# Seven block products for eight in the last MLP layer of a two-layer graph network

## Chip, cores, metric

The kernel runs on one core of a Trainium2 chip. The metric is the device time of one execution in microseconds; the figure given is the median over runs. The profile shown is of one profiled execution.

## The reference

3327 nodes with 1024 features each and a weighted adjacency matrix go through two residual layers. The first normalises the rows, quantises them, multiplies by a quantised weight and then by the adjacency matrix. The second is a graph attention with 8 heads of 64 features, followed by an MLP. Only the end of it is touched here:

```python
enc = jnp.transpose(h, (1, 0, 2)).reshape(x.shape[0], -1)   # 3327 x 512
out = jax.nn.relu(enc @ W1.T + b1)                          # 256
out = jax.nn.relu(out @ W2.T + b2)                          # 256
out = jax.nn.relu(out @ W3.T + b3)                          # 512
out = out @ W4.T + b4                                       # 1024
...
x = x + _L1_gnn_ref(h, adj, ...)
```

All of it is float32. The last product is 3327 x 512 times 512 x 1024, and its result is added to the layer's input, which the kernel calls x1.

## The kernel before

**Stages.** The kernel works through the network in stages: the first layer's support, its product with the adjacency matrix together with the heads of the second layer, the attention (`acc`, `mps`, lines 785 to 1156), and the MLP (lines 1159 to 1257). The nodes lie in 26 tiles of 128 rows, the last with 127 real ones. The MLP takes them in groups of four tiles: six groups of four and one of two.

**A layer of the MLP.** `dense` (line 1166) keeps the features on the partitions and has the nodes of a group as up to 512 columns. For each of the layers h1, h2, h3 TensorE multiplies 128 x 128 blocks of the weight with the group's activations (8, 4 and 8 matmuls), and ScalarE takes each sum out of PSUM with bias and relu (line 1186). Group 0 has its first layer computed inside the last step of the attention.

**The last layer.** `rows_out` (line 1200) makes the output rows of one node tile. Here `h3` is the stationary side (128 features by 128 nodes) and `w4` the moving one (128 by 512 outputs), so the result has nodes on the partitions. Two column halves of 512 and four blocks of features make 8 matmuls. VectorE adds the bias `bb4` to the rows of x1 (line 1201), and then the sums in PSUM to that (line 1205); SyncE's queue sends the rows out (line 1207). A tile's two halves share one PSUM tile of two banks, and there are two such tiles; only the last node tile is taken by halves.

**The order of the work.** The matmuls of the next group's layers h1, h2, h3 are placed between the last-layer products of the current group's tiles by the loop at line 1236, so that ScalarE's activations are done before TensorE needs them. x1 for the next group comes from memory by `load_x1` into one of two buffers, `nodes0` and `nodes1`; `joined` loads the attention's output by a transposing DMA and puts its two 16-bit halves together with four ScalarE copies a group (`enct`, line 1197). Engines take their instructions strictly from a list that a scheduler has ordered at build time: what stands later in an engine's list waits for what stands earlier.

**The seam between attention and MLP.** The last reader of the attention's mask is `sel` (line 1109) on VectorE. Then the last head is closed (lines 924 to 969): sums and a division on VectorE (`su`, L936, L941, L943; `rs`, L946), scaling and an exponential on ScalarE (L939, L949, L951, L952), a last VectorE step `ht` (L956), ScalarE's copy `eh` (L962), and two DMAs to `enc_d` that GpSimd's queue issues (L964). In the same microseconds TensorE computes h2 and h3 of group 0 and ScalarE takes them out.

**Buffers.** `weights` holds the four weights, `rest` the biases and group 0's first layer with its input `enct0`, and `mask1` is the attention's second mask, which is no longer read when the MLP runs.

The softmax here doesn't subtract the row's maximum and nothing guards it: scores larger than these inputs give would overflow.

## Time and profile before

| What | Value |
|---|---|
| Time, median of 3 runs (lowest to highest) | 2207.7 us (2207.35 to 2208.68) |
| Span of the profiled execution | 2207.1 us |
| Clock granted to TensorE | full, mean 1.000 |
| First matmul of h2, group 0 | 1918.2 us |
| First weight load of the last layer | 1929.0 us |
| Last matmul ends | about 2202.6 us |
| 2010 to 2160 us: busy, in us of 150 | PE 150.00, DVE 30.76, ACT 25.17, POOL 0.00 |
| The same stretch, data moved | 85 GB/s |

The profiled execution is known by its span, from the first instruction to the last; the median of the runs lies 0.6 us above it. PE is TensorE, PEld its weight loads, DVE VectorE, ACT ScalarE, POOL GpSimd, SP SyncE. The page gives each engine's busy time, then the span in 40 slices (a digit is the busy share in tenths), then the chain that ended last, followed back from the last instruction, and the costliest groups of instructions: line, engine, operation, output and inputs, shape and count, then busy time and the mean duration in ns, then the engine's idle time ahead of them with what ended it. The timeline gives start and duration in us and the same names. Ends of matmuls are modelled, so their spacing says more than their duration. What the prediction shows of these is not repeated here.

### The profile page before, as it was taken

How to read it: one execution, taken by the hardware profiler on the slowest of the kernel's cores; microseconds unless marked ns; L12 is line 12 of the kernel's file. 1: busy time of each engine (PE TensorE's matmuls, PEld its weight loads, DVE VectorE, ACT ScalarE, POOL GpSimd, SP SyncE). 2: the span in 40 equal slices, each digit the busy share in tenths (PEclk: the TensorE clock that was granted, in tenths of full speed). 3: DMA queues.
4: the chain of work that ended last, by engine and by line, in shares of the span. 5: the costliest groups of instructions: out<-in, count | busy, mean ns of one | idle time of the engine just before them, and what ended most of it. 6: DMA issues, size and time to landing. Idle time of an engine off the chain costs nothing.

```text
span 2207.1 us, 31283 instructions
## 1 busy us (share of the span) xinstructions
PE 2173.1 (98%) x12457; PEld 1747.8 (79%) x12457; DVE 1542.5 (70%) x2000; ACT 1112.0 (50%) x1715; POOL 176.2 (8%) x269
## 2 busy tenths in 40 slices
PE   5999999999999999999999999999999999999999
PEld 2477777776777777799999999999999999744444
DVE  8745555555455555779999999999999999822211
ACT  6734445544455444566555565555555555532110
POOL 2301000111101101100000000000000000000000
PEclk9999999999999999999999999999999999999999
DMA  6654565555655556944242422644242432372221
GB/s 219 165 186 152 160 193 179 171 168 158 185 186 179 164 159 187 322 126 148 87 150 79 146 87 74 221 146 148 85 150 87 138 91 78 103 209 86 97 84 67
DMA packets 242433, 321.13 MB, mean 145 GB/s; under 512 B 104868, under 2 KB 186996, under 8 KB 242288
## 3 DMA queue, kind: packets, MB, share of 16 engines
q1 hardware_dynamic: 221676, 245.91, 36.6%
q0 software_dynamic: 20544, 73.18, 10.6%
q8 instruction: 97, 1.59, 0.3%
q14 instruction: 48, 0.39, 0.1%
q10 hardware_dynamic: 68, 0.06, 0.0%
HBM read 208.72 MB, written 86.79 MB: 134 GB/s over the span
## 4 chain that ended last, share of the span: by engine, by line
PE 89%; DVE 5%; DMA 3%; ACT 1%; issue 1%; SPq 0%; POOL 0%; DVEq 0%; ACTq 0%; POOLq 0%
PE acc L1134 29%; PE mm L730 24%; PE mps L883 15%; PE o L1216 8%; PE whm L641 7%; PE h_ps L1176 5%; PE mm L337 2%; DMA at<-in_adj_t 1%; DMA yht<-yh 1%; DVE sel L1109 1%; DMA xqt<-xq 0%; DVE stats L250 0%; DVE lo L189 0%; DMA w<-in_w 0%; PE o_half L1216 0%
## 5 line engine op out<-in xcount | busy, mean ns | idle before, releaser
L1109 DVE SCALAR_TENSOR_TENSOR sel<-srow,ndst,mask 128x896 fp32r<-128x896 f32 (+1 forms) x832 | 865.2, 1084 | 40.4 <-PE acc L1134 34.8
L883 PE MATMUL mps<-dw,mf 128*128 128x260 f32 x2704 | 453.7, 283 | 0.0
L730 PE MATMUL mm<-s_int,hi 128*128 128x512 f32 x1352 | 426.3, 396 | 0.0
L730 PE MATMUL mm<-s_int,lo 128*128 128x512 f32 x1352 | 416.6, 389 | 0.0
L1134 PE MATMUL acc<-f_even,sel 128*128 128x260 f32 x2704 | 396.8, 284 | 0.7 <-DVE sel L1109 0.7
L1134 PE MATMUL acc<-f_odd,sel 128*128 128x260 f32 x2704 | 394.1, 286 | 0.4 <-DVE sel L1109 0.4
L876 ACT CAST mf<-mask 128x1664 fp32r<-128x1664 uint8 x208 | 331.5, 1594 | 112.6 <-PE mps L883 98.3
L883 PEld LDWEIGHTS mps<-dw,mf 128*128 128x128 f32 x2704 | 377.9, 188 | 0.2 <-ACT part L897 0.2
L1134 PEld LDWEIGHTS acc<-f_odd,sel 128*128 128x128 f32 x2704 | 352.8, 188 | 7.8 <-issue 3.4
L1134 PEld LDWEIGHTS acc<-f_even,sel 128*128 128x128 f32 x2704 | 354.8, 188 | 4.2 <-DVE sel L1109 1.3
L730 PEld LDWEIGHTS mm<-s_int,hi 128*128 128x128 f32 x1352 | 253.9, 188 | 62.5 <-issue 11.5
L730 PEld LDWEIGHTS mm<-s_int,lo 128*128 128x128 f32 x1352 | 253.7, 188 | 52.9 <-DVE lo L189 0.2
L189 DVE TENSOR_TENSOR lo<-at,hi 128x896 fp32r<-128x896 f32 x104 | 106.2, 1021 | 157.3 <-ACT hi L185 157.3
L641 PE MATMUL whm<-whead,ht 128*128 128x512 f32 x416 | 182.7, 592 | 0.0
L1216 PE MATMUL o<-weights,h 128*128 128x512 f32 x400 | 174.8, 592 | 0.0
L190 DVE TENSOR_SCALAR mk<-at 128x896 uint8<-128x896 f32 (+1 forms) x104 | 61.5, 593 | 142.9 <-DMA at<-in_adj_t 142.9
L185 ACT CAST hi<-at 128x896 fp32r<-128x896 f32 x104 | 92.2, 887 | 130.1 <-PE mm L730 94.8
L1216 PEld LDWEIGHTS o<-weights,h 128*128 128x128 f32 x400 | 76.0, 190 | 94.4 <-issue 94.0
L641 PEld LDWEIGHTS whm<-whead,ht 128*128 128x128 f32 x416 | 78.8, 190 | 89.1 <-issue 87.1
L897 ACT COPY part<-mps 128x260 f32<-128x260 f32 x103 | 39.0, 378 | 190.1 <-PE mps L883 190.1
L964 POOL DMA_DIRECT2D enc_d<-eh x64 | 57.6, 903 | 907.0 <-ACT eh L962 906.5
L1186 ACT ACTIVATE h<-h_ps,rest 128x512 f32<-128x512 f32 (+1 forms) x54 | 34.9, 653 | 180.5 <-PE h_ps L1176 180.5
(175 smaller groups left out, 1676.4 us busy)
## 6 DMA issues: line engine op xcount, KB each, us to landing
feat_d<-fw POOLq DMA_DIRECT2D x26, 1040.0 KB, 5.3
f_even<-feat_d SPq DMA_DIRECT2D x7, 3380.0 KB, 13.5
f_odd<-feat_d SPq DMA_DIRECT2D x7, 3380.0 KB, 12.7
at<-in_adj_t SPq DMA_DIRECT2D x52, 448.0 KB, 4.2
at<-in_adj_t SPq DMA_DIRECT2D x52, 384.0 KB, 4.1
dw<-dsum_d SPq DMA_DIRECT2D x16, 910.0 KB, 8.8
dsum_d<-dw POOLq DMA_DIRECT2D x26, 520.0 KB, 6.2
x_d<-xt POOLq DMA_DIRECT2D x26, 512.0 KB, 6.7
```

Source lines behind the costliest of these rows:

```text
L185: ins = nc.scalar.copy(hi, at)
L189: nc.vector.tensor_tensor(lo, at, hi.bitcast(F32), ALU.subtract)
L190: ins = nc.vector.tensor_scalar(mk[:, r], at, 0.0, None, ALU.is_gt)
L641: ins = nc.tensor.matmul(whm, ht[:, k, :], whead[:, k, :], start=(k == 0), stop=(k == KF - 1))
L730: nc.tensor.matmul(mm[:, c * 512 : (c + 1) * 512], which[:, q, :], s_int[j][:, c * 512 : (c + 1) * 512], start=(j == 0 and which is hi), s ...
L876: ins = nc.scalar.copy(mf, mask[:, j : j + TH, :])
L883: nc.tensor.matmul(ps, mf[:, j % TH, :], dw[:, j, :], start=(j == 0), stop=(j == T - 1))
L964: nc.gpsimd.dma_start(enc_d[q, sub[0] * P : (sub[-1] + 1) * P, h * HD : (h + 1) * HD].rearrange("(b p) d -> p b d", p=P), eh[:, q].rearran ...
L1109: ins = nc.vector.scalar_tensor_tensor(sel[:, :nb], srow[:, :nb], ndst[:, j, h : h + 1], mask[:, :, j, :], ALU.is_gt, ALU.mult,)
L1134: ins = nc.tensor.matmul(accs[b], sel[:, b, :], f[:, j, :], start=(j == 0), stop=(j == T - 1))
L1176: ins = nc.tensor.matmul(pss[m][:, :cols], wt[:, k, m * P : (m + 1) * P], xt[:, k, :cols], start=(k == 0), stop=(k == k_n - 1),)
L1216: nc.tensor.matmul(ps, h3[:, k, q * P : (q + 1) * P], w4[:, k, cs], start=(k == 0), stop=(k == D3 // P - 1),)
```

## The change

The last layer is computed for two node tiles at once. The two tiles' features, split in two halves of 256, make a 2 x 2 block matrix (a11, a12; a21, a22); the weight, split in two halves of features and two of outputs, makes another. Their product by Winograd's form of Strassen's scheme needs seven block products and fifteen block sums in place of eight products.

- Four block sums of the weight are made once, by GpSimd, 128 x 1024 elements each: t1 over a quarter of `w4` itself, t2, t3, t4 in the memory of `mask1`. Each takes the one before it, or is ordered with it by the place it overwrites.
- Four block sums of the features are made for each group by VectorE (`combined`), s1 to s4, 512 columns each, in the memory of `enct0`; one set of buffers for all groups.
- A product is two matmuls into one PSUM bank of 512 columns. There are four banks in rotation in place of two tiles of two.
- Seven block sums join the products to output blocks, in `rows_out`: VectorE adds into the x1 rows or into `kept`, three of the products are first copied out of PSUM by ScalarE. Rows leave in halves of 512 columns, four DMAs a pair in place of two.
- The next group's layers stand at other places, between the products of a pair (`at`).

```diff
-    ) as ps_p, tc.tile_pool(name="s4_o", bufs=2, space=PSUM, reuse_waits="tile") as o_ps:
+    ) as ps_p, tc.tile_pool(name="s4_o", bufs=4, space=PSUM, reuse_waits="tile") as o_ps:
...
-        def rows_out(t, x1, h3, q, halfway=lambda: None):
-            nc.vector.tensor_tensor(x1[:, q, :], x1[:, q, :], bb4, ALU.add)
-            yo = s4.tile([P, F], F32, name="yo")
-
-            def leave(c, sums):
-                nc.vector.tensor_tensor(yo[:, c], sums, x1[:, q, c], ALU.add)
+        w4c = [[w4[:, 2 * k : 2 * k + 2, c * 512 : (c + 1) * 512] for c in range(FC)] for k in range(2)]
+        t2, t3, t4 = (
+            masks[1].rearrange("p b j i -> p (b j i)").bitcast(F32)[:, n * F : (n + 1) * F].rearrange(
+                "p (k c) -> p k c", k=2
+            )
+            for n in range(3)
+        )
+        t1 = w4c[0][1]
+        nc.gpsimd.tensor_tensor(t3, w4c[1][1], w4c[0][1], ALU.subtract)
+        nc.gpsimd.tensor_tensor(t1, w4c[0][1], w4c[0][0], ALU.subtract)
+        nc.gpsimd.tensor_tensor(t2, w4c[1][1], t1, ALU.subtract)
+        nc.gpsimd.tensor_tensor(t4, w4c[1][0], t2, ALU.subtract)
+        sums = enct0.rearrange("p k c -> p (k c)").rearrange(
+            "p (s k t i) -> p s k t i", s=4, k=2, t=2
+        )
+
+        def combined(h3, n):
+
+            at = h3[:, :, : 2 * n * P].rearrange("p k (t e i) -> p k t e i", e=2, i=P)
+            (a11, a21), (a12, a22) = [[at[:, 2 * k : 2 * k + 2, :, e] for e in range(2)] for k in range(2)]
+            s1, s2, s3, s4_ = (sums[:, q, :, :n] for q in range(4))
+            nc.vector.tensor_tensor(s1, a21, a22, ALU.add)
+            nc.vector.tensor_tensor(s2, s1, a11, ALU.subtract)
+            nc.vector.tensor_tensor(s3, a11, a21, ALU.subtract)
+            nc.vector.tensor_tensor(s4_, a12, s2, ALU.subtract)
+            return {
+                "1": (a11, w4c[0][0]),
+                "2": (a12, w4c[1][0]),
+                "3": (s4_, w4c[1][1]),
+                "4": (a22, t4),
+                "5": (s1, t1),
+                "6": (s2, t2),
+                "7": (s3, t3),
+            }
+
+        def rows_out(tiles, x1, of, q, gaps):
...
+            for e in range(2):
+                nc.vector.tensor_tensor(x0[:, e], x0[:, e], bb4, ALU.add)
...
+            yo = [s4.tile([P, F], F32, name="yo", bufs=3) for _ in tiles]
+
+            def leave(e, c, one, other):
+                t, cs = tiles[e], slice(c * 512, (c + 1) * 512)
+                nc.vector.tensor_tensor(yo[e][:, cs], one, other, ALU.add)
                 for queue, r in zip((nc.sync, nc.scalar), row_pieces(t)):
...
+                    queue.dma_start(out[t * P + r.start : t * P + r.stop, cs], yo[e][r, cs])
+
+            kept = {b: s4.tile([P, 512], F32, name="p" + b, bufs=1) for b in "165"}
+            for n, b in enumerate("1426573"):
+                st, mv = of[b]
+                ps = o_ps.tile([P, 512], F32, tag="o", name="o")
+                for k in range(2):
+                    nc.tensor.matmul(ps, st[:, k, q // 2], mv[:, k], start=(k == 0), stop=(k == 1))
+                if b in kept:
+                    nc.scalar.copy(kept[b], ps)
+                if b == "4":
+                    nc.vector.tensor_tensor(x21, x21, ps, ALU.add)
+                elif b == "2":
+                    nc.vector.tensor_tensor(x11, x11, ps, ALU.add)
+                    leave(0, 0, kept["1"], x11)
+                elif b == "6":
+                    nc.vector.tensor_tensor(kept["6"], kept["6"], kept["1"], ALU.add)
+                    nc.vector.tensor_tensor(x12, x12, kept["6"], ALU.add)
+                elif b == "5":
+                    nc.vector.tensor_tensor(x12, x12, kept["5"], ALU.add)
+                    nc.vector.tensor_tensor(x22, x22, kept["5"], ALU.add)
+                elif b == "7":
+                    nc.vector.tensor_tensor(kept["6"], kept["6"], ps, ALU.add)
+                    leave(1, 0, kept["6"], x21)
+                    leave(1, 1, kept["6"], x22)
+                elif b == "3":
+                    leave(0, 1, ps, x12)
+                if n in gaps:
+                    gaps[n]()
...
+            of = combined(h3, len(tiles) // 2)
...
+            at = [(0, 6), (1, 2), (1, 5)] if g == 0 else [(0, 2), (0, 6), (1, 2)]
+            for pair in range(len(tiles) // 2):
+                gaps = {n: next_layer for p, n in at if following and p == pair}
+                rows_out(tiles[2 * pair : 2 * pair + 2], enc_x1[g % 2][1], of, 2 * pair, gaps)
```

In the order that the scheduler gives the changed program, GpSimd's four sums stand ahead of the last two `enc_d` DMAs, and ScalarE's eight `enct` copies of groups 1 and 2 ahead of its copy of product 6 of the first pair.

More of the change, by code (lines that the diff above doesn't have):

```diff
@@ L1198, in joined @@
             return xt
-        def rows_out(t, x1, h3, q, halfway=lambda: None):
-            nc.vector.tensor_tensor(x1[:, q, :], x1[:, q, :], bb4, ALU.add)
-            yo = s4.tile([P, F], F32, name="yo")
-            def leave(c, sums):
-                nc.vector.tensor_tensor(yo[:, c], sums, x1[:, q, c], ALU.add)
-                for queue, r in zip((nc.sync, nc.scalar), row_pieces(t)):
-                    queue.dma_start(out[t * P + r.start : t * P + r.stop, c], yo[r, c])
-            by_halves = t == T - 1
-            whole = None if by_halves else o_ps.tile([P, F], F32, name="o")
-            for c in range(FC):
-                cs = slice(c * 512, (c + 1) * 512)
-                ps = ps_p.tile([P, 512], F32, tag="ps", name="o_half") if by_halves else whole[:, cs]
-                for k in range(D3 // P):
-                    nc.tensor.matmul(
-                        ps,
-                        h3[:, k, q * P : (q + 1) * P],
-                        w4[:, k, cs],
-                        start=(k == 0),
-                        stop=(k == D3 // P - 1),
-                    )
-                if c == 0:
-                    halfway()
-                if by_halves:
-                    leave(cs, ps)
-            if not by_halves:
-                leave(slice(0, F), whole)
@@ new lines, in rows_out @@
+        def rows_out(tiles, x1, of, q, gaps):
+            x0 = x1[:, q : q + 2]
+            for e in range(2):
+                nc.vector.tensor_tensor(x0[:, e], x0[:, e], bb4, ALU.add)
+            (x11, x12), (x21, x22) = [
+                [x0[:, e, c * 512 : (c + 1) * 512] for c in range(FC)] for e in range(2)
+            ]
+            yo = [s4.tile([P, F], F32, name="yo", bufs=3) for _ in tiles]
+            def leave(e, c, one, other):
+                t, cs = tiles[e], slice(c * 512, (c + 1) * 512)
+                nc.vector.tensor_tensor(yo[e][:, cs], one, other, ALU.add)
+                for queue, r in zip((nc.sync, nc.scalar), row_pieces(t)):
+                    queue.dma_start(out[t * P + r.start : t * P + r.stop, cs], yo[e][r, cs])
[26 more added lines that the diff above has]
+                    gaps[n]()
@@ L1236, in two_layer_kernel @@
         for g, tiles in enumerate(groups):
-            following = [None] * 4
+            following = []
             if g + 1 < len(groups):
@@ L1241, in two_layer_kernel, with next_layer @@
                     encs[g + 2] = joined(g + 2)
-                layers = [(w1, bb1, "h1"), (w2, bb2, "h2"), (w3, bb3, "h3")]
-                following = [None] * (g == 0) + layers + [None] * (g > 0)
+                following = [(w1, bb1, "h1"), (w2, bb2, "h2"), (w3, bb3, "h3")]
                 h = encs.pop(g + 1)
-            for q, t in enumerate(tiles):
-                def next_layer():
-                    nonlocal h
-                    if following[q] is not None:
-                        wt, bt, tag = following[q]
-                        h = dense(h, wt, bt, len(groups[g + 1]) * P, tag)
-                last = q == len(tiles) - 1
-                rows_out(t, enc_x1[g % 2][1], h3, q, *([next_layer] if last else []))
-                if not last:
-                    next_layer()
+            of = combined(h3, len(tiles) // 2)
+            def next_layer():
+                nonlocal h
+                wt, bt, tag = following.pop(0)
+                h = dense(h, wt, bt, len(groups[g + 1]) * P, tag)
+            at = [(0, 6), (1, 2), (1, 5)] if g == 0 else [(0, 2), (0, 6), (1, 2)]
+            for pair in range(len(tiles) // 2):
+                gaps = {n: next_layer for p, n in at if following and p == pair}
+                rows_out(tiles[2 * pair : 2 * pair + 2], enc_x1[g % 2][1], of, 2 * pair, gaps)
             h3 = h
```

## The prediction

> **What bounds the kernel now.** I read the shares of busy time first, then the same by slices, to see which stage has which limit.

> ```profile
> PE 2173.1 (98%) x12457; PEld 1747.8 (79%) x12457; DVE 1542.5 (70%) x2000; ACT 1112.0 (50%) x1715; POOL 176.2 (8%) x269
> ...
> PE   5999999999999999999999999999999999999999
> ...
> DVE  8745555555455555779999999999999999822211
> ```

> The last five slices are the MLP (1918 us to the end): TensorE full, VectorE at 1 to 2 tenths; GpSimd's line has only zeros there. The chain of waits, in order of time, shows that this stage is TensorE alone, with one short detour at its start:

> ```profile
> 1917.01 2.27 DVE nodes L1201 x2
> 1920.56 1.29 ACT su L939 x5
> 1922.47 7.13 PE h_ps L1176 x16
> 1929.61 13.73 PE o L1216 x32
> ```

> From 1922.47 to 2202.6 no other engine appears. Two things are read here. Work taken from TensorE in this stage shortens the run one for one as long as nothing new makes it wait. And the price of a matmul is the spacing, 13.73 / 32 = 0.429 us a record, not the mean of 592 ns that the row of `o` in the groups gives, since matmuls overlap. A matmul of this fp32 stage leaves two records (208 in the program, 400 + 16 in the trace), so one costs 0.858 us.

> The groups of this stage give the prices on VectorE and, behind the last bar, its idle time and who ended it:

> ```profile
> L1201 DVE TENSOR_TENSOR nodes<-nodes,rest 128x1024 f32<-128x1024 f32 x26 | 31.7, 1224 | 92.4 <-DMA nodes<-x_d 92.4
> L1205 DVE TENSOR_TENSOR yo<-o,nodes 128x1024 f32<-128x1024 f32 x25 | 30.6, 1223 | 120.5 <-PE o L1216 120.4
> ...
> L1205 DVE TENSOR_TENSOR yo<-o_half,nodes 128x512 f32<-128x512 f32 x2 | 1.4, 691 | 5.0 <-PE o_half L1216 5.0
> ```

> The start of the stage is the delicate place. Its timeline, engine by engine (start, duration, engine, line; idle time in brackets):

> ```profile
> 1916.93 2.35 DVE L1201 TENSOR_TENSOR nodes<-nodes,rest 128x1024 f32<-128x1024 f32 x2
> 1919.30 0.97 DVE L936 TENSOR_TENSOR su<-xs 128x780 f32<-128x780 f32 x1
> ...
> 1926.50 0.56 DVE L956 SCALAR_TENSOR_TENSOR ht<-ex,ht 128x384 f32<-128x384 f32 x1 [2.78 <-ACT ex L952]
> ...
> 1927.09 0.83 ACT L962 COPY eh<-ht 128x768 uint16<-128x768 uint16 x1 [0.63 <-DVE ht L956]
> 1927.83 2.50 ACT L1186 ACTIVATE h<-h_ps,rest 128x512 f32<-128x512 f32 x4
> 1938.76 9.72 ACT L1197 COPY enct<-nodes 128x1024 uint16<-128x1024 uint16 x8 [8.43 <-DMA nodes<-enc_d]
> ...
> 1928.22 1.65 POOL L964 DMA_DIRECT2D enc_d<-eh  x2 [11.72 <-ACT eh L962]
> ```

> The reader is to see a chain without slack: VectorE's last step of the attention (L956), ScalarE's copy `eh` right behind it, the four activations that make `h3` right behind that, and TensorE's first `o` weight load at 1929.02. A second chain runs from the write of `eh` (1928.22) through the transposing loads to the copies `enct` (1938.76), which the next group's first layer needs; the first four are done at 1943.6, and that layer starts its matmuls at 1943.2.

> [...]

> ```profile
> 62.84 1.24 DVE L355 TENSOR_SCALAR s_int<-sb 128x1024 fp32r<-128x1024 uint8 x2
> ...
> 63.08 1.04 POOL L287 TENSOR_SCALAR l0v<-mv 128x2 f32<-128x2 f32 x1 [29.39 <-DVE mv L257]
> ```

> The POOL instruction, 0.22 us when undisturbed (88.29), ends just after VectorE's two back-to-back ones, at 64.1 us. It got in at the first gap, not between them. [...]

> **TensorE: removed.** A pair of node tiles took 16 matmuls and takes 14. Thirteen pairs: 26 x 0.858 = 22.3 us less.

> **VectorE and ScalarE: added.** Per pair: two bias adds of 1.22, eleven 512-wide adds of 0.69 (one for product 4, two for 2, two for 6, two for 5, three for 7, one for 3), and half of four operand sums of 0.69. That is 2.4 + 7.6 + 1.4 = 11.4 us. TensorE's lap for a pair of a full group is 14 matmuls and half of the 20 of the layers, 24 x 0.858 = 20.6 us. Hidden by TensorE, with 9 us to spare. If VectorE stood still over 9 us in each lap the cover would be gone; its waits for x1 (92.4 us over 21, 4.4 each, two a pair, 8.8) come close if all lie bare. But in the changed order a bias add for the next group stands behind the previous pair's sums, whose banks are then free; TensorE first needs a bank from behind that add some 19 us later (h2, three products, h3, two products). I cost it at nothing. ScalarE gains three copies of 0.69 a pair beside some 15 us idle: nothing, except at the start. SyncE issues four outputs of half the size for two; 0.34 us each, nothing.

> **GpSimd: added, at the start.** Four adds in a chain, t3, t1, t2, t4. They wait for the last reader of the mask, the `sel` that ends at 1917.0, and stand in the queue ahead of the last two `enc_d` writes. The second product needs t4. Alone: 1917.1 + 9.2 = 1926.3, early enough for everything. With the exclusion:
> - [...] t3 runs 1919.3 to 1921.6; VectorE's chain moves by 2.3, ending L946, which ended at 1923.7 before, at 1926.0. t1 finds it idle, 1925.8 to 1928.1, t2 follows to 1930.5. L956, ready at 1928.8, is held to 1930.5 and ends at 1931.1 instead of 1927.06: 4.0 late. t4 ends at 1933.4.
> - `eh` and then the `h3` activations come 4.0 late, so the first product starts at 1933.0: **4.0 us**. t4 is then in time for the second (1934.7).
> - The `enc_d` write follows t4: 1933.5, 5.3 late. The `enct` copies begin at 1944.1. Seven products end at 1933.0 + 12.0 = 1945.0, and the first layer needs four copies at 1.22 apiece, the fourth at 1949.0 where it would be wanted at 1947.6: **1.4 us**.
> - ScalarE's queue has all eight `enct` copies ahead of the copy of product 6. They end at 1953.8, that copy at 1954.5. The next pair's first product reuses the bank of product 6 (four banks), and would start at 1953.3: **1.2 us**.

> Together 6.6 us. Unhindered GpSimd leaves only the last kind: copies end 1948.5, bank free 1949.2, wanted at 1947.9: 1.3 us. If the two engines alternate strictly from the first instruction on, VectorE loses all 9.2 us of GpSimd's and L956 is some 9.4 late; with the bank's 1.2 that makes 10.6. I take 6.6 since the record at 63.08 shows entry at gaps.

> **Tail: added.** Before, half an add (0.69) follows the last matmul. After, product 7's three adds are still running when product 3 ends 1.7 us later: 2.1 - 1.7 + 0.69 = 1.05, and one more issue. I take 0.5 more.

> Sum: -22.3 + 6.6 + 0.5 = -15.2. Against the profiled span of 2207.1 that is 2191.9; the median of the runs lies 0.6 above the span: **2192.5 us**.

> **Rivals.**
> - *GpSimd is not hindered* (chance 0.22): -22.3 + 1.3 + 0.5, 2187.2 us. For it: no two-input add against a two-input add is in this trace.
> - *The engines alternate* (0.15): -22.3 + 10.6 + 0.5, 2196.5 us. For it: both have work queued from 1917.0; against: the record at 63.08.
> - *VectorE becomes the pace of the PSUM banks* (0.08), the slower side. Its lap of 11.4 plus the x1 waits must pass TensorE's. It decides from 20.6 + 15.2 / 13 = 21.8 us, that is, from waits of 10.4 a pair. With waits of 11.6 the lap is 23.0, and twelve laps lose 2.4 each: 2192.5 + 28.8 = 2221 us. Against: the waits reckoned 8.8, and the 19 us of lead.
> - *Small stalls eat the gain* (0.05): 1 us in each pair, 2205.5, no change that can be told.

> The likeliest, at 0.50, is my own. What a measurement of this kernel tells from no change is about 0.2%, 4.4 us. The first three cases are faster, with a little of the last: 0.88; same 0.04; slower 0.08. The range takes in the unhindered case and the alternating one with 2.5 us more for either: 2185 to 2199.

> **What would show it.** `o` with 364 records at the same spacing, and 24 matmuls a pair in the middle of the stage without gaps: the 22.3. VectorE at some 5 to 6 tenths there. On GpSimd four adds, and beside them VectorE's L936 to L956 stretched; TensorE waiting for ScalarE's `h` before the first product, then for `enct`, then for the copy of product 6. It is wrong if the four adds end before 1927, if TensorE waits for VectorE in the later groups, or if records of `o` are spaced more than 0.43 us.

## The result, and the profile after

The changed kernel takes 2197.2 us (median of 4 runs, 2196.4 to 2197.7) against 2207.5 for the kernel before (4 runs, 2207.2 to 2208.7). The ratio is 0.995, with a 95% interval of 0.9936 to 0.9964: 10.3 us faster, where 15.2 had been expected, or 2192.5.

The page of the changed kernel, shares of busy time and then VectorE by slices:

```profile
PE 2154.9 (98%) x12405; PEld 1738.8 (79%) x12405; DVE 1627.1 (74%) x2144; ACT 1135.0 (52%) x1754; POOL 189.1 (9%) x273
...
DVE  8845555554555555789999999999999999965445
```

TensorE has 52 records fewer (12457 before), all of `o`. VectorE's last five slices went from 2 and 1 to between 4 and 6. So the change did what it says. The chain of waits (start, duration, engine, tile, line) shows where part of the gain stayed:

```profile
1918.94 3.02 DVE su L936
1921.95 3.28 DVE nodes L1239
1925.23 2.62 DVE su L941
...
1936.69 3.03 PE o L1256 x4
...
2014.77 12.02 PE o L1256 x28
...
2055.97 12.02 PE o L1256 x28
```

The last two lines are the same place in two successive groups: a lap of 41.20 us. Before, the laps were 44.63 (2012.01, 2056.64, 2101.28 in the same view). That is 3.43 us for each full group, and with six and a half groups 22.3 us, the whole of the expected saving. The first three lines are longer or new: before, the chain went through VectorE here for 2.27 us of bias adds and 0.98 of L936, and from 1922.47 on it was TensorE alone. Now it goes through small steps of the attention (L936, L941) and bias adds (L1239), and each takes about three to five times its time. The timeline shows why (start, duration, engine, line, operation; in brackets the idle time before and its cause):

```profile
1936.69 3.02 PE L1256 MATMUL o<-weights,h 128*128 128x512 f32 x4 [3.87 <-ACT h L1186]
...
1921.88 3.36 DVE L1239 TENSOR_TENSOR nodes<-nodes,rest 128x1024 f32<-128x1024 f32 x1
...
1934.62 0.56 DVE L956 SCALAR_TENSOR_TENSOR ht<-ex,ht 128x384 f32<-128x384 f32 x1 [2.78 <-ACT ex L952]
...
1916.74 4.39 POOL L1208 TENSOR_TENSOR mask<-weights 128x1024 f32<-128x1024 f32 x1 [0.60 <-DVE sel L1109]
1921.21 2.95 POOL L1209 TENSOR_TENSOR weights<-weights 128x1024 f32<-128x1024 f32 x1
1924.23 3.20 POOL L1210 TENSOR_TENSOR mask<-weights 128x1024 f32<-128x1024 f32 x1
1927.52 2.54 POOL L1211 TENSOR_TENSOR mask<-weights,mask 128x1024 f32<-128x1024 f32 x1
```

Read the four starts of GpSimd's adds (1916.74, 1921.21, 1924.23, 1927.52) against VectorE's entries in the chain. GpSimd's first add ends at 1921.13. The second ends 2.2 us after the VectorE instruction that it waited for (1924.16 and 1921.96), and the same 2.2 us put the first one's entry at 1918.92, when VectorE's two bias adds ended. From there the engines took turns, one instruction each: L936 is 3.02 us long (0.97 before), the third bias add 3.36 (1.22), L941 2.70 (0.56), the fourth bias add 3.36. Each is longer by 2.05 to 2.14 us, 8.5 in all. L956 comes 16.8 us after the start of `h2` (1917.84) where it had come 8.3 after it, and the first product 18.85 after it where it had been 11.25. It is 7.6 us late for 8.5, so the chain had 0.9 us of slack.

The stage then loses time in one more place, for which nothing had been expected. Windows of the changed kernel just behind TensorE's stop (busy time and records of PE, PEld, DVE, ACT and POOL, then the granted TensorE clock, the DMA share and GB/s):

```profile
1938.00:1940.00 2.00, 2.00 (x3) 0.79 (x3) 1.53 (x3) 0.63 (x2) 0.02 (x1) 0.50 0.40 66
```

The clock is 0.50; in the same view it is 1.00 again from 1942 on. At the halved clock records follow each other at 0.853 us instead of 0.429. The way from the first product to the next group's first layer is 28 records, 12.01 us at full clock, and took 13.81.

The sum, against the kernel before: first product 7.6 us late, halved clock 1.8, the next pair's first product 0.5 late (7.35 us after the layer's start, where 6.87 are work), so 9.9 at the start of the stage. At the end TensorE stops at 2189.9 and the span ends at 2195.4, 5.5 later, where it had been 4.5: 1.0. Then -22.3 + 9.9 + 1.0 = -11.4. The spans differ by 11.7, the changed kernel having entered the stage 0.36 us earlier. The medians differ by 10.3 only, since the profiled execution of the kernel before was a long one: runs of this study take some 1.8 us more than their span (2197.31 and 2195.4, for instance), which would put it at 2208.9, 1.4 above its median.

### The profile page after: what moved, and what is told of

Its sections match the earlier page's. It is cut to its first block, busy times and chain, and to the rows that moved or that the text cites. A ratio compares the mean times of both kernels' runs of the same rounds, so it can differ in the third digit from the quotient of the medians.

```text
span 2195.4 us, 31473 instructions
## 1 busy us (share of the span) xinstructions
PE 2154.9 (98%) x12405; PEld 1738.8 (79%) x12405; DVE 1627.1 (74%) x2144; ACT 1135.0 (52%) x1754; POOL 189.1 (9%) x273
## 3 DMA queue, kind: packets, MB, share of 16 engines
q0 software_dynamic: 20544, 73.18, 10.6%
## 4 chain that ended last, share of the span: by engine, by line
PE 86%; DVE 6%; DMA 5%; ACT 2%; issue 1%; SPq 0%; POOL 0%; DVEq 0%; ACTq 0%; POOLq 0%
PE acc L1134 29%; PE mm L730 22%; PE mps L883 15%; PE o L1256 7%; PE whm L641 6%; PE h_ps L1176 4%; PE mm L337 3%; DMA at<-in_adj_t 2%; DMA yht<-yh 2%; DVE lo L189 1%; DMA w<-in_w 0%; ACT enct L1197 0%; DVE prod L655 0%; DVE stats L141 0%; DVE fw L697 0%
## 5 line engine op out<-in xcount | busy, mean ns | idle before, releaser
L964 POOL DMA_DIRECT2D enc_d<-eh x64 | 57.6, 904 | 901.6 <-ACT eh L962 901.1
L612 ACT COPY ht<-yht 128x1024 uint16<-128x1024 uint16 x50 | 67.7, 1355 | 72.8 <-DMA yht<-yh 72.8
L337 PE MATMUL mm<-w_int,xqt 128*128 128x512 bf16 x416 | 94.4, 383 | 6.6 <-DVE w_int L468 4.5
L648 ACT ACTIVATE wht<-whm,lnr 128x512 f32<-128x512 f32 x26 | 18.0, 691 | 144.4 <-PE whm L641 138.0
## 6 DMA issues: line engine op xcount, KB each, us to landing
f_even<-feat_d SPq DMA_DIRECT2D x7, 3380.0 KB, 13.8
```

The lines of the kernel that those rows point to most:

```text
L337: nc.tensor.matmul(mms[t][:, r], xqts[t][:, k, :], w_int[:, k, r], start=(k == 0), stop=(k == KF - 1))
L612: nc.scalar.copy(halves_of_words(ht[:, c * KF // FC : (c + 1) * KF // FC].rearrange("p k i -> p (k i)")), yht.rearrange("p (two k) i -> p ...
```

## The experiments

**The theory** after the result: GpSimd's adds and VectorE's two-input operations exclude each other, and *take turns*, so that each add costs VectorE's chain its full 2.1 us. Rivals: the adds only hold up what stands behind them in GpSimd's own queue (the last `enc_d` writes) and the products that read them; or VectorE's own added work is what comes late. All runs carry a kernel before of their own on the same chip (2208.7 to 2209.3), and the ratios are to that.

**1. No sums.** The four adds are left out; products 4 to 7 take unsummed blocks of `w4`.

```diff
-        t2, t3, t4 = (masks[1]...)
+        t2, t3, t4 = w4c[1][1], w4c[0][1], w4c[1][0]
-        nc.gpsimd.tensor_tensor(t3, w4c[1][1], w4c[0][1], ALU.subtract)
...
```

> The four weight sums are left out; products 4, 6 and 7 take unsummed blocks of w4, so the numbers that come out are not the layer's. Everything else of the changed kernel stands. Theory 'exclusion' (GpSimd's two-input adds hold up VectorE's L936 to L956, with them eh, the h3 activations and the first product): the first product starts at about 1929.2 instead of 1936.7, only the wait for product 6's copy is left, about 8 us less than the changed kernel: 2189. Rival 'queue' (GpSimd's adds cost because product 4 waits for t4 and the enc_d writes stand behind them): the same, 2189. Rival 'work' (the added adds, copies and outputs eat the gain, the weight sums nothing): 2196 to 2197.

Measured: 2187.8 us, ratio 0.9906 [0.9892, 0.9921]. L936 is 0.97 us long, L956 comes 8.3 us after the start of `h2`, the first product 11.3. VectorE's added work in all later pairs is still there. So the sums at the start cost the changed kernel about 9 us. And VectorE's own work costs no more than the tail: 22.3 less the tail's 1.0 and a wait of 0.47 us at product 6's bank are 20.8, and this run is 21.0 below its kernel before (the interval of its ratio allows 17 to 24).

**2. Memsets in their place.** GpSimd is kept busy for as long and longer, in the same place of its queue, by instructions that write and don't read. The products take the unsummed blocks and zeros.

```diff
-        nc.gpsimd.tensor_tensor(t3, w4c[1][1], w4c[0][1], ALU.subtract)
...
+        for first in (0, 512, 0, 512, 0):
+            nc.gpsimd.memset(flat[:, first : first + 2560], 0.0)
```

> GpSimd's four adds are replaced by five memsets of 128x2560 over the same memory, about 12 us, at the same place of its queue: as long, but reading nothing. t1 to t4 are then not the weight's sums, so the output isn't the layer's. Exclusion: VectorE's L936 to L956 keep the durations of the kernel before (0.97, 1.22, 0.56), L956 starts at about 1926.2, the first product at about 1929.2; the enc_d writes about 1 us late: 2189 to 2191. Queue: nothing changes against the changed kernel, 2197.

Measured: 2187.8, ratio 0.9909 [0.9893, 0.9926], 1.2 below the range: the `enc_d` writes, expected 1 us late, are 0.2 late. Timeline of this kernel:

```profile
1917.69 0.97 DVE L936 TENSOR_TENSOR su<-xs 128x780 f32<-128x780 f32 x1
...
1915.47 11.38 POOL L1210 MEMSET mask<- 128x2560 f32 x5 [0.58 <-DVE sel L1109]
```

GpSimd works until 1926.85 with VectorE beside it, and L936 is not stretched. The queue as the cause falls; in the changed kernel too the adds are done at 1930.06, and the `enc_d` write behind them then waits 6.28 us for `eh`. So VectorE's two-input operations are stretched by 2.05 to 2.14 us each beside the adds, which read, and by nothing beside the memsets, which only write: L936, L941 and the bias adds take 0.97, 0.56 and 1.22 us here, as in the kernel before.

**3. The sums in the kernel before.** Nothing else of the change is in it, and nobody reads them.

```diff
+        nc.gpsimd.tensor_tensor(t3, w4c[1][1], w4c[0][1], ALU.subtract)
+        nc.gpsimd.tensor_tensor(t1, w4c[0][1], w4c[0][0], ALU.subtract)
...
```

> The kernel before with GpSimd's four weight sums added at the place where the change has them, all four written to mask1 and read by nobody; the output is the layer's. Exclusion: L956 some 8 us late, TensorE's first last-layer matmul with it, 2215 to 2217. Queue: no product waits for t4, only the enc_d writes come late and have cover: 2207.5 to 2209. Work: 2207.5.

Measured: 2218.3, ratio 1.0045 [1.003, 1.006], 9.6 us slower and 1.3 above the range. Its timeline:

```profile
1918.03 3.02 DVE L936 TENSOR_TENSOR su<-xs 128x780 f32<-128x780 f32 x1
```

The same 3.02 as in the changed kernel, and L956 at 1933.72. No product waits for a sum here, so the loss is the stretched chain and what follows from it, two halvings of TensorE's clock among it (0.50 in 1924 to 1926 and in 1936 to 1938).

**4. The sums on VectorE.** They take the place of the first group's four bias adds, which go behind L956.

```diff
-        nc.gpsimd.tensor_tensor(t3, w4c[1][1], w4c[0][1], ALU.subtract)
...
+        nc.vector.tensor_tensor(t3, w4c[1][1], w4c[0][1], ALU.subtract)
...
-            for e in range(2):
-                nc.vector.tensor_tensor(x0[:, e], x0[:, e], bb4, ALU.add)
+            with tc.issue_after(closed[0].ins) if tiles[0] < 4 else nullcontext():
+                for e in range(2):
+                    nc.vector.tensor_tensor(x0[:, e], x0[:, e], bb4, ALU.add)
```

> The changed kernel with the four weight sums on VectorE, where the four bias adds of group 0 stood, and those bias adds behind L956. VectorE's work ahead of L956 is then as long as in the kernel before. Exclusion: L956 at about 1926.3, first product at about 1929.2, only the wait for product 6's copy left, 2188 to 2190. Queue: about the same, 2189. Work: 2196 to 2197, since nothing is taken away.

Measured: 2188.0, ratio 0.9907 [0.9892, 0.9922]; it beats both kernels, as its interval lies below that of the change (0.9936 to 0.9964). A sum takes VectorE 1.22 us, and the timeline has the last step of the attention on time, 8.4 us after the start of `h2`:

```profile
1925.67 0.56 DVE L956 SCALAR_TENSOR_TENSOR ht<-ex,ht 128x384 f32<-128x384 f32 x1 [2.78 <-ACT ex L952]
```

**5. The bias adds late, the sums on GpSimd.** Only the second half of edit 4. GpSimd does the same work, and fewer VectorE instructions meet it.

> GpSimd keeps the four weight sums; the four bias adds of the first group go behind VectorE's closing ops of the attention (L936, L941, L943, L946, L956). Exclusion with turn-taking: VectorE then has only two or three two-input operations between the releases of GpSimd's adds, so each of L936 and L941 is stretched by at most one GpSimd add (2.2 us): L956 at 1927 to 1930 instead of 1934.6, first product 1930 to 1932 instead of 1936.7, time 2189.5 to 2193. If only GpSimd's total of 9 us counted, in whatever order: L956 still at about 1934 and 2197. If the bias adds alone were the loss (VectorE's own work, no GpSimd): L956 at 1925 and 2188.

Measured: 2191.0, ratio 0.9913 [0.9898, 0.9928]. The timeline:

```profile
1918.75 2.60 DVE L941 TENSOR_TENSOR su<-md,su 128x390 f32<-128x390 f32 x1
1921.46 2.52 DVE L943 TENSOR_TENSOR su<-su 128x390 f32<-128x390 f32 x1
```

Two instructions are stretched, by 2.0 us each, not L936 and L941 as expected but L941 and L943: the first add was over (1917.9) 0.2 us after L936 began. L946, which has one input, takes its 0.19 us at 1924.01 beside GpSimd's fourth add (1923.63 to 1926.18) and isn't stretched. L956 is at 1927.41, inside what turn-taking gave, and the time too. The first product, at 1932.56, is 0.6 later than it gave, with a clock of 0.50 in 1928 to 1930. The same four adds cost 9 us in one order of VectorE's queue and some 3 in the other (2191.0 against 2188.0): what counts is how many instructions of the chain meet an add.

**6. The sums behind the last `enc_d` write.** GpSimd's adds are put behind it, and the bias adds as in 5.

```diff
+        with tc.issue_after(written[0].ins):
+            nc.gpsimd.tensor_tensor(t3, w4c[1][1], w4c[0][1], ALU.subtract)
...
```

> GpSimd's four sums are put behind its last enc_d write, and the first group's four bias adds behind VectorE's L956. Exclusion as the cause: the closing of the attention is undisturbed, L956 at 1925, the enc_d write and TensorE's return on time (first product about 1928.5), but products 4, 6 and 7 wait for t1 to t4, which are done only at about 1936 to 1940 beside s1 to s4 and the bias adds: first wait in product 4 or 6 of pair 0, 5 to 9 us there, part of it filled by nothing; 2192 to 2198. If the loss in the changed kernel came from the waiting products themselves and not from VectorE's stretched operations, this is as slow as it or slower; if from the stretched operations alone, 2189 or below.

Measured: 2200.3, ratio 0.9955 [0.994, 0.997], some 2 us above the range. The attention ends undisturbed (L956 8.3 us after the start of `h2`), but the timeline has the products waiting:

```profile
1935.58 2.08 PE L1258 MATMUL o<-weights,h 128*128 128x512 f32 x2 [4.58 <-POOL weights L1211]
1941.09 3.78 PE L1258 MATMUL o<-mask,h 128*128 128x512 f32 x4 [3.43 <-POOL mask L1213]
```

The two waits are 8.0 us, within the 5 to 9. The first is not where it was expected: the two records before it, the two behind it and ScalarE's copy at 1937.69 are all product 1, whose weight block no sum writes, and yet its second half waits for t1 (L1211). What the expectation left out is the clock, at 0.50 in every window from 1934 to 1946: from the first product to the next group's first layer TensorE takes 24.4 us, 12.0 of work, 8.0 of waits and some 4.4 of halved clock. The expectation also held that a time like the changed kernel's or above it would speak for the waiting products as the cause there. It doesn't: in the changed kernel the first product waits for ScalarE's `h`, 3.87 us, and no product waits for a sum. What this run shows is that waiting for the sums costs as much as stretching the attention.

**7. More work for VectorE in every pair.** On version 4, eight or sixteen adds of 128x512 per pair into a scratch tile that nobody reads.

```diff
+            junk = s4.tile([P, 512], F32, name="junk", bufs=1)
+            for _ in range(8):
+                nc.vector.tensor_tensor(junk, x22, bb4[:, :512], ALU.add)
```

> Built on the version with the weight sums on VectorE (2188.0); eight more adds 128x512 into a scratch tile per pair, read by nobody. VectorE hidden under TensorE: 11.4 + 8 x 0.69 = 16.9 us per pair against a lap of 20.6, so no change, 2187 to 2191. VectorE as the pace of the PSUM banks: every pair loses up to 5.5 us, 14 pairs, up to 2265.

> As e7 with sixteen such adds per pair: 11.4 + 16 x 0.69 = 22.4 us against a lap of 20.6. VectorE hidden up to the lap: it is now the longer one and the stage takes 13 x 1.8 = 24 us more, 2205 to 2220. If VectorE had been the pace already: 13 x 11 = 143 us more. If the lap had room that the sum misses (adds overlap): no change, 2188.

Measured: 2191.6 with eight, a little above its range (ratio 0.9916 [0.9901, 0.9931]), and 2209.1 with sixteen (0.9997 [0.9988, 1.0006]). The second lies in its range of 2205 to 2220, but not for the reason given there. The windows with sixteen say that TensorE did not slow down in the middle of the stage:

```profile
2010.00:2130.00 120.00, 120.00 (x281) 53.11 (x280) 118.70 (x182) 32.80 (x48) 0.00 (x0) 1.00 0.31 105
```

VectorE is busy for 118.70 of 120 us and TensorE for all of them, with a lap of still 41.20. The scheduler put scratch adds where they held up nothing that TensorE waits for, and they piled up: with eight, seven of them run after everything else (5.0 us), with sixteen, twenty (14.5 us). From TensorE's last product to the end of the span it is 23.7 us with sixteen and 5.5 in version 4. That is 18.2 of the 21 us that sixteen cost, and 2.1 more are lost in the last, small group; none is lost in a full group's lap, as the expectation had it. VectorE has 9 us a pair to spare, but this test does not show what something *ahead* of the useful adds would do. Experiment 8 does for a wait, unasked.

**8. TensorE kept busy in its stops.** In the changed kernel, two matmuls in the first stop and four in the second, which nobody reads; and the changed kernel again on the same chip.

```diff
+        filled(2)
         h3 = dense(h, w3, bb3, len(groups[0]) * P, "h3", by_input=True)
+        filled(4)
```

> The changed kernel with six matmuls more that nobody reads, two in TensorE's first stop at the start of the last stage (2.4 us) and four in the second (3.9 us), 1.7 and 3.4 us long, so that TensorE has work while it waits. If the halved clock there (0.857 us a record instead of 0.429) follows from TensorE's idleness: spacing 0.429 throughout, the way from the first product to the next layer 12.0 us instead of 13.8, 2195.4 against 2197.2. If it follows from GpSimd's and VectorE's work or from anything else in that place: the same halved records, and 2197 to 2199.

> The changed kernel once more, for a comparison on one chip with e10 and e6: 2197 as before, halved clock after both stops; every theory expects the same here.

Measured: the changed kernel again 2196.6 (ratio 0.9947 [0.9935, 0.996]), the filled one 2205.6 (0.9984 [0.9977, 0.999]), which nothing had led one to expect. The timeline of the filled one, TensorE and then VectorE:

```profile
1951.99 3.78 PE L1256 MATMUL o<-weights,rest 128*128 128x512 f32 x4 [7.38 <-DVE nodes L1260]
...
1950.11 1.23 DVE L1239 TENSOR_TENSOR nodes<-nodes,rest 128x1024 f32<-128x1024 f32 x1 [8.78 <-DMA nodes<-x_d]
1951.26 0.68 DVE L1260 TENSOR_TENSOR nodes<-nodes,o 128x512 f32<-128x512 f32 x1
```

The added matmuls take tiles of the four `o` banks, and in this program the scheduler put the next group's first bias add, which waits for `x_d`, ahead of product 4's add (L1260), which frees the bank that product 5 (1951.99) waits for. TensorE stood still for 7.4 us. In the changed kernel that bias add stands behind the adds of products 4 and 2, waits 4.89 us, and TensorE doesn't notice. Why the scheduler changed the order is not shown. So the time of this run says nothing about the clock. Its records do: after the two stops, now 0.65 and 1.97 us long, the clock is 1.00 in every window from 1920 to 1944 and the records are 0.429 apart; after the new stop of 7.4 us it is 0.50. In the repeat of the changed kernel the first stop of 2.36 us left the clock at 1.00, where the first profile had 0.50 after it, and the longer stop (5.39 us there) halved it again: 13.75 us from the first product to the layer. The expectation had the clock halved after both. In the filled kernel GpSimd's adds ran from 1917.5 to 1930.9 with the clock full, and the halving came at 1947.7 with GpSimd idle, so work on GpSimd is not its cause. In this stage all six traces with a stop of 2.36 us or more (the changed kernel, its repeat and experiments 3, 5, 6 and the filled kernel) have a halving. The timelines of the other seven show no stop above 0.62 us at the start of the stage, and no halving there. That the stops cause it is supported by all these profiles, but not proved by a time.

**9. ScalarE's copies in another order.** Version 4, with the `enct` copies of group 2 behind the copies of products 6 and 5 of the first pair.

```diff
-                if g + 2 < len(groups):
+                if 0 < g < len(groups) - 2:
                     encs[g + 2] = joined(g + 2)
...
+                if g == pair == 0:
+                    with tc.issue_after(copied["5"].ins):
+                        encs[2] = joined(2)
```

> The version with the sums on VectorE (2188.0), and ScalarE's enct copies of group 2 put behind its copies of products 6 and 5 of the first pair. If the 0.5 us that the second pair's first product waits for ScalarE's copy of product 6 comes from the enct copies ahead of it: no wait there, 2187.5. If it comes from the copies of group 1 alone, which stay ahead: unchanged, 2188.

Measured: 2188.0, ratio 0.9907 [0.9894, 0.9921]. The wait for product 6's bank (0.47 us in version 4) is gone from the trace, the first pair's copy done at 1944.9; the time does not show half a microsecond.

## Why the prediction was right or wrong

**TensorE, removed: right to the digit.** 22.3 us expected, 6.5 x 3.43 = 22.3 measured, at a spacing of 0.429 wherever the clock was full.

**VectorE hidden: right.** In 2010 to 2150 us of the changed kernel TensorE is busy for 140.00 of 140 us and VectorE for 73.83, a share of 0.53 where 11.4 in 20.6 had given 0.55. The rival of the slower side needed waits of 10.4 us a pair in front of the bank-freeing adds; bias adds waited 39.5 us for `x_d` in the whole stage. Experiment 8 has a bank freed late by VectorE, though (7.38 us), through the order of its queue, not through the sum of its work.

**The start loss: wrong in its mechanism, 9.9 us for 6.6.** The step that failed is the first of the three under GpSimd: "It got in at the first gap, not between them", read from the record at 63.08 and taken over to four adds in a row. The two back-to-back instructions there, and the two bias adds here, did go first. But once an add was waiting, it came next after the running VectorE instruction, although VectorE's own next one was ready. So four instructions of VectorE were held up by an add each, where the prediction had two delays, of 2.3 and 1.7, and L956 was 8.5 us late for 4.0. That is turn-taking, at 2.05 to 2.14 us a turn, and the prediction had it as a rival, 2196.5 at 0.15, with a start loss of 10.6. It was put aside on one record in which only one GpSimd instruction was waiting. That an add and a two-input operation exclude each other at all was an assumption, and the 2.3 us for an add, from which all the sums under GpSimd start (four make the 9.2), an estimate of the author's; no trace of the kernel before shows either. The changed kernel and experiments 1 to 3 show the first, and the first add of experiment 5 took 2.36 us. So the case that came true is this rival, and the measured time lies in the stated range because the range had been drawn to take the rival in. That 10.6 comes so near 9.9 is in part luck: 1.8 of the 9.9 is a halved clock that neither case had.

**The terms behind it.** Nothing had been put down for TensorE's clock, 1.8. The wait for `enct`, 1.4, did not come, and the clock is the reason: counted from the start of `h2`, the copies began 9.25 us later than before, and the seven products had slipped by 9.4, the 7.6 of the first and the clock's 1.8. The layer's load that waits for the fourth copy is at 1952.65, that copy ended at 1952.58. At full clock the load would have stood at about 1950.9 and waited some 1.7 us (an estimate from these figures), so the halved clock cost this kernel next to nothing on top: it stands where that wait would have stood. The wait for product 6's bank, 1.2, was 0.3 to 0.5. It was 0.47 in experiment 1 too, without contention, where the prediction had 1.3 for that case: it took the next pair's first product as wanted at 1947.9, reckoned from the weight load at 1929.02, and that run, set to the same start of `h2`, puts it at 1948.5.

**The tail and the base.** The tail was 1.0 for 0.5. And the step from span to median, 0.6, should have been 1.8. Start 3.3, tail 0.5 and base 1.2, less 0.36 for the earlier start of the stage, are 4.6 of the 4.7 us by which 2192.5 missed, closer than the intervals allow.

**Unhindered GpSimd** was put at 2187.2; the kernels without contention took 2187.8 to 2188.0.

## What to carry to other kernels

Before work is moved to GpSimd, look at what VectorE does in that place. Here a two-input operation that met one of GpSimd's adds took 1.96 to 2.14 us longer (the changed kernel and experiment 5), nearly the 2.36 us of the add, while beside memsets it took no longer. On a chain that others wait for that made 8.5 us, where the same sums on VectorE took 4 x 1.22 us. A stop of TensorE can cost more than its length: here nine of the ten stops of 2.36 us or more had a clock of 0.50 in them or in the work behind them, which cost the changed kernel 1.8 us; look whether another wait would have filled the same time. And when an engine has time to spare, ask about the order of its queue: here one instruction that waited 8.78 us for a transfer, ahead of one that frees a bank, stopped TensorE for 7.38 us, in a stage where VectorE had been busy for about half of the time (0.53 in the changed kernel).
